# A graph network's neighbour sums: 28 blocks of destinations by matrix product and 21 by gathering, with gathered rows split into three bf16 parts

## The chip, the cores and the metric

The kernel runs on one core of a Trainium2 chip. The time is device microseconds for one execution. Three runs of the kernel before took 2231.62, 2232.75 and 2237.27 us; the median, 2232.75 us, is the time that is compared. The profile is of one further execution.

## The reference

A layer norm and a ReLU turn x (6250 nodes, 256 channels, float32) into h. Then four layers of a graph network follow. Each adds to every node the sum of its neighbours' rows over 100,000 edges (sorted by destination) and applies a three-stage MLP. The last layer's output is added to the input.

```python
def agg(h):
    return jax.ops.segment_sum(h[src], dst, num_segments=N)   # N = 6250
for l in range(NL - 1):                                        # NL = 4
    h = x + agg(x)
    h = jax.nn.relu(h @ W1s[l] + b1s[l])
    h = jax.nn.relu(h @ W2s[l] + b2s[l])
    x = h @ W3s[l] + b3s[l]
h = x + agg(x)
h = jax.nn.relu(h @ cW1 + cb1)
h = jax.nn.relu(h @ cW2 + cb2)                                 # 64 channels
return h @ cW3 + cb3
```

## The kernel before

Nodes are handled in 49 blocks of 128. W1 of a layer is folded into the layer before it (the product of W3 and W1 is made in a preparation of some 145 us), so that the sums are taken over rows that have been multiplied by W1 already, and a layer is: neighbour sums, bias and ReLU, second matrix, bias and ReLU, third matrix, bias.

The neighbour sums of a block of destinations are made in one of two ways.

By product: the lists `panels` name groups of three or four destination blocks. For each panel, a matrix of edge counts (128 sources by 128 destinations for each pair of blocks, kept in DRAM as uint8 in `mats`) is multiplied with all 49 source blocks. The source rows lie in SBUF in `XY` as two float32r halves, a high part and a low part, so that each step (one source block) takes four matmuls: two chunks of channels times two halves (`product`, L1334). Their moving operand is the panel's slice of counts, cast from uint8 by ACT (L1310) or DVE (L1312) into the tile `a`; it is 512 columns wide for four blocks and 384 for three. A panel is 49 such steps. In layer 0 the count matrices are built beside the products out of one-hot matmuls (`build`, L1010), for the panel after the one at work; the last panel, blocks 44 to 47, is not yet there in layer 0.

By gathering: the list `gone` names the blocks that are not in a panel (and blocks 44 to 47, for layer 0 alone). `Gathered.send` (L1183) issues, for each such block, 18 indirect DMAs from GpSimd (L1198). Each brings 128 rows of the layer's table in DRAM, one per edge: nine tiles for each half of 64 destinations. `Gathered.one_hots` makes one-hot matrices of the destinations on DVE (L1223), and `Gathered.add` multiplies them with the rows (L1242). A half of 64 destinations is cut into quarters of 32, following the order of the edges, so that an output of 32 rows is made by a matmul on 32 of TensorE's columns. Rounds pair the tiles of the two quarters; two tiles may belong to both. One call of `add` does three of the six rounds and is called a visit here; a block takes two visits.

Then `finish` adds the block's own row (DVE, L1254), transposes the result (L1264) and hands groups of blocks to `mlp`, as `product` does with its panel. `mlp` spreads its pieces over the following steps with `later` and `due`. The result `zz` is stored to the next layer's table (SP, `rows_io`, L501). Its high and low parts are put in `XY` by `split` (L1055, L1056), directly or after a reload of the row (`back`).

The order on every engine is written out by hand, step by step. `tick` advances one step and runs what is due. A planner spreads the visits over the layer: `when` holds an estimated time for each step, `begin` starts the gathers of a layer as soon as all its table rows have been issued for storing, the first visit comes LEAD units of `when` later, and the last one TAIL steps before the end of the layer. `mlp` keeps its own due time in `free`: a group's second matrix starts at the step after it is handed over or when the group before it leaves room, 5 + (n + 1) // 2 steps apart for the hurried last ones.

Queues: GpSimd issues the gathers; SP issues all other loads and stores of the main part in order (`fetch` L1033, `rows_io` L501 and L506, weights). The gathered rows lie in 24 buffers (layer 0) or 26 (later), and up to two or three visits are sent ahead.

Of the kernel before, what the change touches and what calls it, by code (L numbers as in the profile page):

```python
# [8 lines left out]
F32 = mybir.dt.float32  # L9
# [3 lines left out]
BF16 = mybir.dt.bfloat16  # L13
# [383 lines left out]
def sorted_edges(  # L397
# [57 lines left out]
    CUT = (3, 5)  # L455

    ROUNDS = [(3, 3), (4, 4), (0, 5), (1, 6), (2, 7), (None, 8)]
    EB = -(-E // P)
# [6 lines left out]

    gone = [(0, 4), (4, 4), (8, 4), (12, 4), (16, 3), (44, 4), (48, 1)]
    panels = [(19, 3), (22, 4), (26, 4), (30, 4), (34, 3), (37, 3), (40, 4), (44, 4)]
    S0 = 2 * panels[0][0]
# [21 lines left out]
    eps = const.tile([P, 1], F32, name="eps")  # L490
    tables = [dram.tile([N, C], F32, name=f"table{l}") for l in range(NLAYER + 1)]
    w31d = [dram.tile([P, (KC + 1) * C], F32, name=f"w31_{l}") for l in range(NLAYER)]
    mats = [dram.tile([P, n, NT * P], U8, name=f"mat{p}") for p, (_, n) in enumerate(panels)]
# [407 lines left out]
    with tc.manual_schedule():  # L901
# [36 lines left out]
        def load_weights(l):  # L938
            w2 = load_w("w2", W2s[l] if l < NLAYER else cW2, work, nc.sync)
            if l < NLAYER:  # L940
                w3 = work.tile([P, KC + 1, C], F32, name="w3")
                nc.sync.dma_start(out=w3.rearrange("p k c -> p (k c)"), in_=w31d[l])
            else:
                w3 = late.tile([NOUT, C], F32, name="cw3", bufs=1)
                nc.sync.dma_start(out=w3, in_=cW3)
                row = late.tile([P, C], F32, name="cb3r", bufs=1)
                nc.sync.dma_start(out=row, in_=bass.AP(tensor=cb3.tensor, offset=cb3.offset,
                                                       ap=[[0, P], [1, C]]))
                w3 = (w3, row)
            weights[l] = w2, w3  # L950
# [37 lines left out]
        def build(hots, ats, ps_b):  # L988
# [7 lines left out]
            for k, (p, s, q0) in enumerate(batches):  # L996
# [6 lines left out]
                for q in range(0, BATCH, 2):  # L1003
# [11 lines left out]
                    step += 1  # L1015
                    if step % 4:
                        nc.scalar.copy(o, v)  # L1017
                    else:
                        nc.vector.tensor_copy(o, v)  # L1019
# [22 lines left out]
        def tick():  # L1042
            now[0] += 1
            run = [f for t, f in due if t <= now[0]]
            due[:] = [(t, f) for t, f in due if t > now[0]]
            for f in run:
                f()


# [3 lines left out]
        def split(j, m, z):  # L1053

            nc.scalar.copy(XY[:, j:j + m, :C], z[:, :m, :])  # L1055
            later(1, lambda: nc.vector.tensor_tensor(XY[:, j:j + m, C:], z[:, :m, :],  # L1056
                                                     XY[:, j:j + m, :C].bitcast(F32), OP.subtract))

        def reload(l, j):
# [24 lines left out]
        def mlp(l, b0, n, h1, hurry):  # L1084
# [19 lines left out]
            def third(i):  # L1104
                m = min(2, n - i)
                w3 = weights[l][1]
                if end:
                    xt = late.tile([P, 2, C], F32, name="xt", bufs=3)
                    if b0 + i + m == NT and LAST < P:
# [15 lines left out]
                if end:  # L1125
                    z = late.tile([P, 2, C], F32, name="z", bufs=2)
                    later(2, lambda: nc.vector.tensor_tensor(z[:, :m, :], v, xt[:, :m, :], OP.add))  # L1127
                    later(4, lambda: rows_io(out, b0 + i, m, z, False))
                    return
                z = work.tile([P, 2, C], F32, name="zz", bufs=3)  # L1130
                later(2, lambda: nc.vector.tensor_tensor(  # L1131
                    z[:, :m, :], v, w3[:, KC:, :].to_broadcast([P, m, C]), OP.add))

                def store():
                    rows_io(tables[l + 1], b0 + i, m, z, False)
                    blocks = range(b0 + i, b0 + i + m)
                    kept.update((l, j) for j in blocks)
# [20 lines left out]
        class Gathered:  # L1158
            def __init__(self, l):
                self.l, self.sent, self.done = l, 0, 0  # L1160
                self.first = None
                self.end = ends[l] - TAIL
                self.blocks = [(b, n, i, left[q] + i * T)
                               for q, (b, n) in enumerate(gone) for i in range(n)
                               if l == 0 or (b, n) != panels[-1]]
                self.own = {}
                self.visits = [(g, rounds) for g in range(len(self.blocks)) for rounds in VISITS[l > 0]]
                self.n = len(self.visits)
# [5 lines left out]

            @staticmethod
            def tiles(rounds):
                return sorted({k for r in rounds for k in ROUNDS[r] if k is not None})

            def begin(self, t):
                self.first = when[t] + LEAD  # L1180
                self.pace = (when[self.end] - self.first) / (self.upto[-1] - self.upto[1])

            def send(self, upto):  # L1183
                while self.sent < min(upto, self.n):
# [8 lines left out]
                    for k in self.tiles(rounds):  # L1193
                        for h in range(2):
                            t = gath.tile([P, C], F32, name="rows")
                            self.rows[g, h, k] = t
                            o = self.blocks[g][3] + h * TS + k
                            nc.gpsimd.indirect_dma_start(  # L1198
                                out=t, out_offset=None, in_=tables[self.l][:, :],
                                in_offset=bass.IndirectOffsetOnAxis(ap=idx[:, o:o + 1], axis=0),  # L1200
# [13 lines left out]
            def one_hots(self, v):  # L1214
                g, rounds = self.visits[v]
                o = self.blocks[g][3]
                self.hots = {}
                for r in rounds:
                    hot = work.tile([P, 2, 2, Q], F32, name="hot", bufs=6)
                    for i, k in enumerate(ROUNDS[r]):  # L1220
# [8 lines left out]
            def add(self):  # L1229
# [5 lines left out]
                if v == 0:  # L1235
                    self.one_hots(0)
                end = rounds[-1] == len(ROUNDS) - 1
                for r in rounds:
                    for h in range(2):
                        for m, k in enumerate(ROUNDS[r]):  # L1240
                            if k is not None:
                                nc.tensor.matmul(  # L1242
                                    self.sums[(2 * h + m) * Q:(2 * h + m + 1) * Q, :C],
                                    self.hots[r, m][:, h, :], self.rows[g, h, k], start=(r == 0),
                                    stop=(r == (len(ROUNDS) - 2 if m == 0 else len(ROUNDS) - 1)))
                self.done += 1
# [5 lines left out]
            def finish(self, b, n, g, sums, own):  # L1252
                u = work.tile([P, C], F32, name="u", bufs=1)
                later(1, lambda: nc.vector.tensor_tensor(u, sums[:, :C], own[:, 0, :], OP.add))  # L1254
                if g == 0:
# [27 lines left out]
        ahead = [2, 3]  # L1283
        LEAD, TAIL = 75, 8

        ends = [PRE + NT * sum(k + 1 for k in last[:l + 1]) for l in range(NLAYER + 1)]
        when = [0.0]
        for l, p, _ in units:
            beside = panels[p + 1][1] / 3 if l == 0 and p >= 0 else 0
            when.append(when[-1] + (panels[p][1] + 2 + beside if p >= 0 else 7))  # L1290
        VISITS = [[[0, 1, 2], [3, 4, 5]], [[0, 1, 2], [3, 4, 5]]]
        layers = [Gathered(l) for l in range(NLAYER + 1)]
# [71 lines left out]
        with tc.tile_pool(name="hots", bufs=1) as hots, tc.tile_pool(  # L1364
            name="ats", bufs=1
        ) as ats, tc.tile_pool(name="rings", bufs=AHEAD + 2) as rings, tc.tile_pool(
            name="gath", bufs=24
        ) as gath, tc.tile_pool(
# [17 lines left out]
        late = ctx.enter_context(tc.tile_pool(name="late", bufs=1))  # L1386
        rings = ctx.enter_context(tc.tile_pool(name="rings2", bufs=AHEAD + 4))
        gath = ctx.enter_context(tc.tile_pool(name="gath2", bufs=26))
        ps_a = ctx.enter_context(tc.tile_pool(name="ps_a2", bufs=4, space=PSUM))
# [68 lines left out]
```

## Time and profile before

| | |
|---|---|
| median of three runs | 2232.75 us |
| profiled execution: time / span | 2230.63 us / 2228.8 us |
| TensorE clock granted, mean | 0.983 |
| gathers per layer (0; 1, 2, 3) | 432; 360 |
| products per layer (matmuls; 512 wide / 384 wide) | layer 0: 784 / 588; later: 980 / 588 |
| DMA | 395.56 MB, mean 177 GB/s; queue 0 (GpSimd's) 200.88 MB, 30.2% of 16 engines; queue 1 (SP's) 189.68 MB, 26.8% |
| stages from first gather to last (us) | 144.7 to 713; 746.2 to 1203.5; 1244.4 to 1703; 1741.5 to 2201.5 |
| busy in the stage of layer 1 (457.3 us) | TensorE 450.33, DVE 147.47, ACT 141.91, GpSimd 347.89, DMA share 0.60 |

A line of a group names the code line, the engine, the operation, what is written from what, the shape and the count; then the busy time in us and the mean length in ns of one; then the idle time of the engine just before, and what ended it. A line of a timeline gives the start in us, the length in us, the engine, the line and the operation. PE is TensorE, PEld its weight loads, POOL is GpSimd. An indirect DMA on POOL counts as busy only while it is being issued; its transfer runs on afterwards.

### The profile page before, as it was taken

The numbers are of one execution on the slowest core, as the hardware profiler recorded it, in microseconds if no ns is written. First come the engines' busy times: TensorE is split into PE (matmuls) and PEld (weight loads), VectorE is DVE, ScalarE is ACT, GpSimd is POOL, SyncE is SP. The second block draws the span as 40 slices with busy tenths as digits, with TensorE's granted clock in tenths as the row PEclk, the third lists the DMA queues.
The fourth block names the chain that finished last, engine by engine and source line by source line (L and its number), as shares of the span: only waits on it lengthen the run. The fifth ranks groups of instructions, "written<-read, shape, count | busy, mean of one in ns | idle before, by whom it ended". The sixth has DMA issues, their size and how long they took to land.

```text
span 2228.8 us, 35398 instructions
## 1 busy us (share of the span) xinstructions
PE 2118.0 (95%) x12356; PEld 1559.5 (70%) x12356; DVE 918.2 (41%) x2723; ACT 920.1 (41%) x1915; POOL 1521.5 (68%) x1570
## 2 busy tenths in 40 slices
PE   4778999999999999999999999999999999999998
PEld 2555766667776777778877777778877766677765
DVE  6667465445656522223323422223323423333332
ACT  3666565666667422223334322322324423222222
POOL 2337777777776477777774577777774577777773
PEclk9888999999999999999999999999999999999999
DMA  5436575565666655555655655555655655666663
GB/s 173 134 120 201 185 227 173 178 211 174 200 205 225 195 168 172 165 156 170 193 167 172 191 173 169 157 161 180 187 163 166 204 173 177 184 184 186 191 186 102
DMA packets 264100, 395.56 MB, mean 177 GB/s; under 512 B 36353, under 2 KB 210028, under 8 KB 263912
## 3 DMA queue, kind: packets, MB, share of 16 engines
q0 software_dynamic: 73920, 200.88, 30.2%
q1 hardware_dynamic: 187936, 189.68, 26.8%
q10 hardware_dynamic: 2056, 2.65, 0.4%
q8 instruction: 99, 1.62, 0.3%
q14 instruction: 89, 0.73, 0.1%
HBM read 335.81 MB, written 57.26 MB: 176 GB/s over the span
## 4 chain that ended last, share of the span: by engine, by line
PE 65%; DMA 4%; issue 2%; POOL 1%; ACT 0%; DVE 0%; SPq 0%; POOLq 0%; DVEq 0%
PE agg L1334 45%; PE sums L1242 8%; PE ps L1099 5%; PE ps L1122 4%; DMA rows<-table,idx 3%; POOL rows L1198 1%; PE ps L1119 1%; PE pt L1264 1%; PE bp L1010 1%; DMA xt<-in_x_dram 0%; ACT h L1347 0%; DMA own<-table 0%; DVE z L1127 0%; ACT at L1017 0%; ACT h L1268 0%
## 5 line engine op out<-in xcount | busy, mean ns | idle before, releaser
L1198 POOL DMA_INDIRECT rows<-table,idx x1512 | 1484.3, 982 | 614.0 <-issue 243.5
L1334 PE MATMUL agg<-a,XY 128*128 128x512 f32 (+1 forms) x6076 | 1454.7, 386 | 3.6 <-ACT a L1310 3.2
L1334 PEld LDWEIGHTS agg<-a,XY 128*128 128x128 f32 x6076 | 1085.4, 189 | 239.1 <-issue 81.0
L1310 ACT CAST a<-at 128x512 fp32r<-128x512 uint8 (+1 forms) x943 | 537.0, 579 | 650.3 <-PE agg L1334 585.2
L1312 DVE CAST a<-at 128x512 fp32r<-128x512 uint8 (+1 forms) x576 | 279.6, 490 | 498.7 <-PE agg L1334 455.0
L1242 PE MATMUL sums<-rows,hot 128*32 128x256 f32 x3696 | 281.5, 387 | 31.9 <-DMA rows<-table,idx 30.4
L1242 PEld LDWEIGHTS sums<-rows,hot 128*32 128x32 f32 x3696 | 119.4, 110 | 169.7 <-issue 54.7
L1017 ACT CAST at<-bp 128x392 uint8<-128x392 f32 x348 | 161.1, 490 | 142.8 <-PE bp L1010 139.9
L1099 PE MATMUL ps<-h,w 128*128 128x512 f32 (+5 forms) x392 | 164.3, 541 | 1.2 <-ACT h L1347 1.2
L1254 DVE TENSOR_TENSOR u<-sums,own 128x256 f32<-128x256 f32 x84 | 35.5, 423 | 291.7 <-PE sums L1242 291.7
L1010 PE MATMUL bp<-hi,lo 128*128 128x196 bf16 x928 | 136.0, 259 | 19.9 <-DVE hi L969 11.7
L1223 DVE TENSOR_TENSOR hot<-colf,rel 128x64 f32<-128x64 f32 x924 | 140.6, 217 | 12.3 <-PE sums L1242 11.9
L1122 PE MATMUL ps<-w,h 128*128 128x256 f32 x588 | 140.0, 379 | 0.0
L1010 PEld LDWEIGHTS <-lo 128*128 128x128 bf16 x928 | 71.9, 100 | 94.8 <-issue 43.9
L969 DVE TENSOR_TENSOR lo<-lanes,pairs 128x512 bf16<-128x512 bf16 x232 | 97.1, 419 | 84.0 <-PE bp L1010 58.4
L969 DVE TENSOR_TENSOR hi<-cols,pairs 128x784 bf16<-128x784 bf16 x232 | 129.6, 559 | 0.0
L1122 PEld LDWEIGHTS ps<-w,h 128*128 128x128 f32 x588 | 111.0, 189 | 15.7
L1268 ACT ACTIVATE h<-pt,bias 128x256 f32<-128x256 f32 (+1 forms) x92 | 36.9, 453 | 199.1 <-PE pt L1264 199.1
L1101 ACT ACTIVATE h<-ps,bias 128x512 f32<-128x512 f32 (+5 forms) x98 | 62.4, 637 | 109.6 <-PE ps L1099 109.6
L1131 DVE TENSOR_TENSOR zz<-ps,w 128x512 f32<-128x512 f32 (+1 forms) x81 | 51.7, 638 | 130.9 <-PE ps L1122 130.9
L1099 PEld LDWEIGHTS ps<-h,w 128*128 128x128 f32 (+1 forms) x392 | 68.2, 181 | 51.3 <-issue 29.4
L1019 DVE CAST at<-bp 128x392 uint8<-128x392 f32 x116 | 65.5, 565 | 91.9 <-PE bp L1010 90.3
(134 smaller groups left out, 716.6 us busy)
## 6 DMA issues: line engine op xcount, KB each, us to landing
at<-mat SPq DMA_DIRECT2D x133, 448.0 KB
at<-mat SPq DMA_DIRECT2D x84, 336.0 KB
rows<-table,idx POOLq DMA_INDIRECT x1512
mat<-at SPq DMA_DIRECT2D x29, 784.0 KB
table<-zz SPq DMA_DIRECT2D x66, 256.0 KB
back<-table SPq DMA_DIRECT2D x126, 128.0 KB
own<-table SPq DMA_DIRECT2D x80, 128.0 KB
xs<-in_x_dram SPq DMA_DIRECT2D x8, 768.0 KB
```

The costliest lines, as they stand in the source:

```text
L969: nc.vector.tensor_tensor(o.rearrange("p q (n t) -> p q n t", t=2), values.rearrange("p (n t) -> p n t", t=2)[:, None, :, :].to_broadcast( ...
L1010: nc.tensor.matmul(bp[:, m * HW:(m + 1) * HW], lo[:, q + m, :], hi[:, q + m, :], start=True, stop=True)
L1017: nc.scalar.copy(o, v)
L1019: nc.vector.tensor_copy(o, v)
L1099: nc.tensor.matmul(ps[:mp, :w], weights[l][0][:, c, i * P:i * P + mp], h1[:, c, :w], start=(c == 0), stop=(c == KC - 1))
L1122: nc.tensor.matmul(o, h2[0][:, c, nodes], w3[:, c, :], start=(c == 0), stop=(c == KC - 1))
L1198: nc.gpsimd.indirect_dma_start(out=t, out_offset=None, in_=tables[self.l][:, :], in_offset=bass.IndirectOffsetOnAxis(ap=idx[:, o:o + 1], a ...
L1223: nc.vector.tensor_tensor(hot[:, i, :, :], colf[:, None, i * Q:(i + 1) * Q].to_broadcast([P, 2, Q]), rel[:, o + k:o + k + TS + 1:TS, None] ...
L1242: nc.tensor.matmul(self.sums[(2 * h + m) * Q:(2 * h + m + 1) * Q, :C], self.hots[r, m][:, h, :], self.rows[g, h, k], start=(r == 0), stop= ...
L1310: nc.scalar.copy(o, mat[l, p][j])
L1312: nc.vector.tensor_copy(o, mat[l, p][j])
L1334: nc.tensor.matmul(agg[c][:, :w], XY[:, j, o:o + P], a[:, :w], start=(j == 0 and half == 0), stop=(j == NT - 1 and half == 1))
```

## The change

The blocks are dealt out anew: seven panels of four, blocks 20 to 47, instead of five of four and three of three (19 to 47). Gathered are blocks 0 to 19 and 48 in all layers, and 44 to 47 in layer 0: 25 blocks in layer 0 and 21 in each later one, instead of 24 and 20.

From layer 1 on, the rows that are gathered are no longer float32. When a result `zz` is stored, `in_thirds` also splits each block of it into three bf16 parts (a cast on ACT, a subtraction on DVE, a cast, a subtraction) and stores these, 1.5 KB per row, in a second table `thirds`; `one_step` moves these jobs on at each step, and `finish_thirds` completes them at once where the last results of a layer are stored. A gathered tile is multiplied with one one-hot matrix for 64 destinations, in two bf16 matmuls: the first two parts together (512 columns), then the third (256 columns) on top of the first. A block takes nine rounds, in visits of five and four. DVE adds the two halves of the sum. The one-hot matrices of a visit are made by one instruction. Layer 0 keeps the old way with its float32 rows.

The first visit and the last one of layers 1 to 3 are planned anew (LEAD 90 instead of 75, TAIL 2 instead of 8). The gathered rows lie in 22 buffers, the tiles `a` of the later layers in one buffer less (6 instead of 7 with AHEAD of 3). In the beginning, ACT alone copies the one-hot products out of PSUM.

```diff
-    gone = [(0, 4), (4, 4), (8, 4), (12, 4), (16, 3), (44, 4), (48, 1)]
-    panels = [(19, 3), (22, 4), (26, 4), (30, 4), (34, 3), (37, 3), (40, 4), (44, 4)]
+    gone = [(b, 4) for b in range(0, 20, 4)] + [(44, 4), (48, 1)]
+    panels = [(b, 4) for b in range(20, 48, 4)]
...
+    thirds = [dram.tile([N, 3 * C], BF16, name=f"thirds{l}") for l in range(1, NLAYER + 1)]
...
-                    if step % 4:
+                    if step % 4 or step <= 2 * PRE:
                         nc.scalar.copy(o, v)
...
             for f in run:
                 f()
+            one_step()
...
+        def in_thirds(l, j, z, of):
+            tri = work.tile([P, 1, 3 * C], BF16, name="tri", bufs=2)
+            t = [tri[:, 0, i * C:(i + 1) * C] for i in range(3)]
+            nc.scalar.copy(t[0], z)
+            yield
+            left = work.tile([P, C], F32, name="left", bufs=1)
+            nc.vector.tensor_tensor(left, z, t[0], OP.subtract)
+            yield
+            nc.scalar.copy(t[1], left)
+            yield
+            nc.vector.tensor_tensor(t[2], left, t[1], OP.subtract)
+            rows_io(thirds[l - 1], j, 1, tri, False)
+
+        def one_step():
+            for a in list(thirding):
+                a[1] += 1
+                if next(a[0], True):
+                    thirding.remove(a)
+            if waiting and (not thirding or thirding[-1][1] > 2):
+                a = waiting.pop(0)
+                job = in_thirds(*a)
+                next(job)
+                thirding.append([job, 1, a[3]])
+
+        def finish_thirds(upto):
+            while any(a[-1] <= upto for a in thirding + waiting):
+                one_step()
...
                 def store():
+                    blocks = range(b0 + i, b0 + i + m)
+                    waiting.extend((l + 1, j, z[:, j - b0 - i, :], of) for j in blocks)
+                    if hurry:
+                        finish_thirds(of)
                     rows_io(tables[l + 1], b0 + i, m, z, False)
...
-                self.end = ends[l] - TAIL
+                self.end = ends[l] - (TAIL if l else 8)
...
+                self.rounds = [(k,) for k in range(TS)] if l else ROUNDS
...
-                self.first = when[t] + LEAD
+                self.first = when[t] + (LEAD if self.l else 75)
...
-                            t = gath.tile([P, C], F32, name="rows")
+                            if self.l:
+                                t = gath.tile([P, 3 * C], BF16, name="rows")
+                            else:
+                                t = gath.tile([P, C], F32, name="rows")
...
-                                out=t, out_offset=None, in_=tables[self.l][:, :],
+                                out=t, out_offset=None,
+                                in_=thirds[self.l - 1][:, :] if self.l else tables[0][:, :],
...
+                            if self.l:
+
+                                nc.tensor.matmul(o, self.hots[r, m][:, h, :], t[:, :2 * C],
+                                                 start=(r == 0), stop=False)
+                                nc.tensor.matmul(o[:, :C], self.hots[r, m][:, h, :], t[:, 2 * C:],
+                                                 start=False, stop=stop)
...
-        LEAD, TAIL = 75, 8
+        LEAD, TAIL = 90, 2
...
-        VISITS = [[[0, 1, 2], [3, 4, 5]], [[0, 1, 2], [3, 4, 5]]]
+        VISITS = [[[0, 1, 2], [3, 4, 5]], [[0, 1, 2, 3, 4], [5, 6, 7, 8]]]
...
-            name="gath", bufs=24
+            name="gath", bufs=22
...
-        rings = ctx.enter_context(tc.tile_pool(name="rings2", bufs=AHEAD + 4))
-        gath = ctx.enter_context(tc.tile_pool(name="gath2", bufs=26))
+        rings = ctx.enter_context(tc.tile_pool(name="rings2", bufs=AHEAD + 3))
+        gath = ctx.enter_context(tc.tile_pool(name="gath2", bufs=22))
```

## The prediction

> **What bounds the kernel now.** I read the busy shares first, then the groups kept apart by shape:
>
> ```profile
> PE 2118.0 (95%) x12356; PEld 1559.5 (70%) x12356; DVE 918.2 (41%) x2723; ACT 920.1 (41%) x1915; POOL 1521.5 (68%) x1570
> L1198 POOL DMA_INDIRECT rows<-table,idx x1512 | 1484.3, 982 | 614.0 <-issue 243.5 <-DMA own<-table 112.9 <-PE agg L1334 90.8
> L1334 PE MATMUL agg<-a,XY 128*128 128x512 f32 x3724 | 978.1, 409 | 0.3
> L1334 PE MATMUL agg<-a,XY 128*128 128x384 f32 x2352 | 477.7, 352 | 3.4 <-ACT a L1310 3.2
> L1242 PE MATMUL sums<-rows,hot 128*32 128x256 f32 x3696 | 281.5, 387 | 31.9 <-DMA rows<-table,idx 30.4
> ```
>
> TensorE is busy 95%, GpSimd 68%. The 68% hides a second full engine, as the timeline of GpSimd at the end of layer 0 and of layer 1 shows (start, length, idle before):
>
> ```profile
> 710.63 0.95 POOL L1198 DMA_INDIRECT rows<-table,idx  x1 [0.30 <-issue]
> 711.89 0.95 POOL L1198 DMA_INDIRECT rows<-table,idx  x1 [0.30 <-issue]
> 746.21 0.95 POOL L1198 DMA_INDIRECT rows<-table,idx  x1 [33.38 <-DMA own<-table]
> 747.47 0.95 POOL L1198 DMA_INDIRECT rows<-table,idx  x1 [0.30 <-issue]
> ...
> 1202.48 1.03 POOL L1198 DMA_INDIRECT rows<-table,idx  x1 [0.30 <-issue]
> 1244.45 0.95 POOL L1198 DMA_INDIRECT rows<-table,idx  x1 [40.94 <-DMA own<-table]
> ```
>
> Every gather has 0.30 us before it, whatever releaser is named, so its true price is 1.26 us, and they follow without a pause except at the layer changes. Layer 0: 432 gathers from 144.7 to 711.9, 567.2 us (1.316 each, some stretched). Layers 1 to 3: 360 each, from 746.2, 1244.45 and 1741.6, in 456.3, 457.6 and 458.8 us (up to 1.278 each). With the breaks of 34.3, 42.0 and 39.6 us and 28.4 us from the last gather to the end, the chain of gathers is the whole span: 144.7 + 567.2 + 34.3 + 456.3 + 42.0 + 457.6 + 39.6 + 458.8 + 28.4 = 2228.9. What room GpSimd has is seen where the last gathered matmuls ("visits") of layers 1 and 3 start:
>
> ```profile
> 1217.61 1.50 PE L1242 MATMUL sums<-rows,hot 128*32 128x256 f32 x20
> 2200.42 1.14 POOL L1198 DMA_INDIRECT rows<-table,idx  x1 [0.30 <-PE agg L1334]
> 2202.95 1.62 PE L1242 MATMUL sums<-rows,hot 128*32 128x256 f32 x20
> ```
>
> Layer 1's starts 15.1 us after its last gather, layer 3's 2.5 us, about the flight time; the same subtraction gives 7.2 in layer 0 and 12.5 in layer 2. With 3 us for the flight GpSimd can spare some 4, 12, 10 and 0 us. Both engines are near their limit.
>
> **Gathers, by GpSimd.** Blocks gathered rise from 24 to 25 in layer 0 and from 20 to 21 in the others, at 18 gathers each: 72 more, 1584. Layer 0: 449 periods x 1.316 = 590.9 us. The later ones fetch 1.5 KB per row instead of 1 KB. Near rows, with 98 rows of 1 KB, 72 rows of 0.5 KB, and 98 rows of 5.5 KB:
>
> ```profile
> 40.44 0.97 POOL L680 DMA_INDIRECT wds<-split_e,starts  x1 [0.30 <-issue]
> 71.03 0.95 POOL L741 DMA_INDIRECT near_i<-in_src_dram,from_i  x1 [0.31 <-issue]
> 13.42 1.55 POOL L649 DMA_INDIRECT near_i<-in_dst_dram,at_i  x1 [9.61 <-DVE at_i L628]
> ```
>
> Half a KB costs 0.02 us at most between the first two; the third, an estimate by a straight line, gives (1.55 - 0.97) x 0.5 / 4.5 = 0.06. I take today's 1.275 (1.258 and 1.335 are the ends): 377 x 1.275 = 480.7 us per layer. The Trainium skill, DMA: Bandwidth & Descriptors, section "Issuing engines are not separate DMA queues", says that starting a DMA is usually small beside the DMA itself. Here it isn't: queue 0's 30.2% of the span is 673 us for 1512 gathers, 0.445 us of all engines each against 1.26 of issue. By the rule the gathers would cost what they transfer, 0.67 us at 1.5 times the bytes, still hidden, and the sum would be TensorE's alone; by the row it is GpSimd's. I go by the row. The DMA engines' share, 0.59 to 0.61 in these stages, would rise by 378 x 0.67 / 521 - 360 x 0.445 / 498 = 16 points, and 6 for the thirds' writes: near 80%, not a bound, but flights may lengthen.
>
> **The breaks.** From a last visit to the next first gather takes 27.1, 26.8 and 27.0 us today: 16 steps of the product, the MLPs of block 48 and of the last panel, the store and its flight. In layers 1 and 2 TAIL of 2 puts the visit 6 steps later, but the MLP of block 48 then pushes that of the last panel 6 steps into the next layer: again 16 steps. All are now four blocks wide; eight were three: 32 matmuls x 0.06 = 1.9 us more. The last blocks must also be written as thirds before the next gather: cast, subtract, cast, subtract at some 0.41 us each (the rows of L1055 and L1056), two blocks staggered by three steps of this chain, ahead of the table's store on SP: about 7 x 0.41 = 3 us and a second store in SP's queue and in flight, 5 in all (1 to 8). GpSimd's first gather waits for both, and behind the casts stand the panel's own casts on ACT and DVE. A break thus costs, without slack, 3 + 27 + 1.9 + 5 = 37 us. The tail: 25.9 us today from visit to end; six steps x 4 x 0.237 = 5.7 less, block 48's MLP no longer covered, 1.5 more, 3 of flight: 24.7.
>
> **Sum along GpSimd:** 144.7 + 590.9 + 37 + 480.7 + 37 + 480.7 + 37 + 480.7 + 24.7 = 2313.4.
>
> **TensorE.** The products, from the longest stretches:
>
> ```profile
> 829.45 9.62 PE L1334 MATMUL agg<-a,XY 128*128 128x512 f32 x40
> 1240.28 10.76 PE L1334 MATMUL agg<-a,XY 128*128 128x384 f32 x60
> 604.61 0.51 PE L1010 MATMUL bp<-hi,lo 128*128 128x196 bf16 x4
> ```
>
> Without the last one's drain, 0.237 and 0.177 us apiece. A later layer: 980 x 0.237 + 588 x 0.177 = 336.3 today, 7 panels x 196 x 0.237 = 325.2 after, 11 less; the same in layer 0. Visits today: 1.43 us to the next product's start and 0.09 of the wait before, 1.52, two per block, 3.04; 20 blocks 60.8. A visit of 24 matmuls takes 1.50 us, like one of 20: three rounds in which four groups of 32 columns run side by side. After, each of 18 tiles takes a 512- and a 256-wide bf16 matmul on 64 columns; bf16 runs at 85 ns per 196 columns (0.51 less 0.34 for two, halved), so 0.22 and 0.11. The Trainium skill, TensorEngine Tiling (Array Packing), Theoretical Speedup, allows up to 2 times for 64 columns: 18 x 0.33 / 2 = 2.97, with 0.3 per visit of entry and exit 3.6 per block. But TensorE: Matmul & The Clock Gate, "The mechanism", has matmuls start strictly in order, and the code issues both of one half before the other's: the 256-wide one waits for its own columns and holds the other half back. Then a tile pair takes 2 x 0.22, nine of them 3.96, with exits 4.57. No row has such pairs; I take 4.57, since today's starts are in order too: 21 x 4.57 = 96.0, 35 more per layer (15 by the first rule). A layer of 497.6 us (the mean of two between first gathers), less 4 of waits, becomes 518. GpSimd needs 480.7 + 37 = 517.7.
>
> So both chains ask for the same, and since neither can run far ahead (22 row buffers, 28 gathers in three visits), they cost each other something: today 497.6 where GpSimd alone without slack needs 457 + 30 = 487 and TensorE 494. I add 5 per layer: 2313.4 + 15 = 2328. The measured median lies 3.95 above the span (the profiled execution itself 1.8): **2332 us**.
>
> **At nothing:** one block less to build saves 32 bf16 matmuls (3 us) in layer 0, where the visits wait for gathers anyway; uncovered it is a gain of 3. The thirds' casts within a layer, 49 blocks x 2 x 0.41 = 40 us each on ACT and DVE, fit: these are busy 142 and 147 of 457 us; if they delay a panel's casts, TensorE pays some us. The fewer and wider one-hots lighten DVE. Weights moved from one pool to another, and smaller pools, move no work.
>
> **Rivals.**
> - *Cheap ends.* The price stays at 1.258, thirds hide in the break, the two halves overlap: 2313 - 0.017 x 1131 - 12 + 4 = 2286. For it: the undisturbed period; against: a DMA load near 80%.
> - *Dearer gathers.* 1.335: 2313 + 0.06 x 1131 + 4 = 2385. For it: the 5.5 KB row; against: the flat rows.
> - *TensorE alone, halves don't overlap.* 18 x 0.33 + 0.6 = 6.5 per block: a layer of 518 + 21 x 2 = 560, in all some 2332 + 3 x 38 = 2446. Against: the rounds of four.
> - *Faster.* TensorE is the only bound and the 72 gathers vanish in GpSimd's idle stretches: 2233 - 44 of products + 7 of visits (63 x 3.0 - 60 x 3.04) = 2196. For it: 116 us of breaks and 12 to 15 us before the last visits. It decides from the point where 91 us of gathers fit; I find 26 of slack and 4 in the tail. If the breaks are dependences, as the store before each first gather says, it falls.
>
> **How the numbers follow.** Forecast 0.55 (2305 to 2355); cheap ends 0.20; dearer gathers 0.13; no overlap 0.06; faster 0.04; the change of no effect within the 0.3% that a measurement of this kernel can tell 0.02. The range 2275 to 2390 takes in the first three. Faster 0.04, same 0.02, slower 0.94.
>
> **What would show it.** Right: GpSimd's gathers 1.26 to 1.28 apart in unbroken rows of 378, breaks of 35 to 40 us, last visits 3 to 5 us behind the last gather, TensorE's waits for rows well above 30.4 us, most in layer 0. Wrong: gathers that pause within a layer (TensorE bounds), a period other than 1.26, visits of 3 or 6 us, breaks under 30.

## The result, and the profile after

The changed kernel takes 2350.85 us (median of four runs, 2346.46 to 2354.27), the kernel before 2233.82 us beside it: 1.0521 times, with a 95% interval of 1.0498 to 1.0545. The forecast was 2332 us. The profiled execution took 2349.53 us, its span 2347.7.

The busy shares and the groups of the profile after, in the same columns as before:

```profile
PE 2157.4 (92%) x11192; PEld 1490.3 (63%) x11192; DVE 979.2 (42%) x2438; ACT 980.2 (42%) x2072; POOL 1624.4 (69%) x1642
...
L1247 POOL DMA_INDIRECT rows<-thirds,idx x1134 | 1126.7, 994 | 455.4 <-issue 177.1
L1411 PE MATMUL agg<-a,XY 128*128 128x512 f32 x5292 | 1419.1, 414 | 14.0 <-ACT a L1387 13.4
...
L1247 POOL DMA_INDIRECT rows<-table,idx x450 | 460.5, 1023 | 178.4 <-issue 72.2
...
L1310 PE MATMUL sums<-rows,hot 128*64 128x512 bf16 x1134 | 226.8, 386 | 73.0 <-DMA rows<-thirds,idx 71.8
...
L1312 PE MATMUL sums<-rows,hot 128*64 128x256 bf16 x1134 | 180.0, 274 | 0.0
...
L1315 PE MATMUL sums<-rows,hot 128*32 128x256 f32 x1100 | 92.3, 402 | 17.3 <-DMA rows<-table,idx 17.3
```

TensorE is less busy than before (92% against 95%), in a longer span, and it waits for gathered rows 71.8 + 17.3 = 89.1 us, where it was 30.4. GpSimd's share hardly moved, from 68% to 69%: an undisturbed gather counts as busy for 0.95 us of its 1.26, so that even an unbroken chain of gathers shows only three quarters. Its timeline at the end of layer 1 (start, length, idle before):

```profile
1268.32 1.13 POOL L1247 DMA_INDIRECT rows<-thirds,idx  x1 [0.30 <-issue]
1269.77 0.95 POOL L1247 DMA_INDIRECT rows<-thirds,idx  x1 [0.32 <-issue]
1306.97 1.10 POOL L1247 DMA_INDIRECT rows<-thirds,idx  x1 [36.25 <-DMA back<-table]
1308.37 1.18 POOL L1247 DMA_INDIRECT rows<-thirds,idx  x1 [0.30 <-PE agg L1411]
```

The chain of gathers, laid out as in the prediction from the starts of the first and last gather of each layer, is again the whole span. The last column is after minus before:

| part of the chain | before | predicted | after | after - before |
|---|---|---|---|---|
| to the first gather | 144.7 | 144.7 | 144.6 | -0.1 |
| layer 0: 432, then 450 gathers | 567.2 | 590.9 | 596.4 | +29.2 |
| layers 1 to 3: 360, then 378 gathers each | 456.3, 457.6, 458.8 | 480.7 each | 490.5, 489.3, 489.5 | +96.6 |
| three breaks | 34.3, 42.0, 39.6 | 37 each | 38.3, 37.2, 37.4 | -3.0 |
| last gather to the end | 28.4 | 24.7 | 24.6 | -3.8 |
| sum (span) | 2228.9 | 2313.4 | 2347.8 | +118.9 |

The 72 further gathers at the old mean price (18 at 1.316 us, 54 at 1.275) are 92.5 us of the 118.9. The other 33 us within the layers are nearly all gathers that became longer. The breaks and the end gave 7 us back.

One circumstance of the experiments: in the first ten the kernel before itself took 2857 to 2868 us, because every engine paused again and again there, mostly at the issue of instructions, so these ten are compared as ratios to the kernel before beside them; in the last two it took 2235.06 us.

### The profile page after: what moved, and what is told of

The parts are those of the page before. It is cut to its first block, busy times and chain, and to the rows that moved or that the text cites. A ratio compares the mean times of both kernels' runs of the same rounds, so it can differ in the third digit from the quotient of the medians.

```text
span 2347.7 us, 33135 instructions
## 1 busy us (share of the span) xinstructions
PE 2157.4 (92%) x11192; PEld 1490.3 (63%) x11192; DVE 979.2 (42%) x2438; ACT 980.2 (42%) x2072; POOL 1624.4 (69%) x1642
## 3 DMA queue, kind: packets, MB, share of 16 engines
q10 hardware_dynamic: 2056, 2.65, 0.3%
## 4 chain that ended last, share of the span: by engine, by line
PE 67%; DMA 17%; ACT 4%; issue 4%; DVE 4%; POOL 3%; SPq 0%; ACTq 0%; DVEq 0%; POOLq 0%
PE agg L1411 41%; DMA rows<-thirds,idx 11%; PE ps L1141 6%; PE ps L1164 5%; PE sums L1310 5%; POOL rows L1247 3%; PE sums L1315 2%; DMA thirds<-tri 2%; PE bp L1013 2%; PE sums L1312 2%; DMA rows<-table,idx 1%; PE bp L869 1%; ACT a L1387 1%; ACT at L1020 1%; PE pt L1341 1%
## 5 line engine op out<-in xcount | busy, mean ns | idle before, releaser
L1247 POOL DMA_INDIRECT rows<-thirds,idx x1134 | 1126.7, 994 | 455.4 <-issue 177.1
L1411 PE MATMUL agg<-a,XY 128*128 128x512 f32 x5292 | 1419.1, 414 | 14.0 <-ACT a L1387 13.4
L1387 ACT CAST a<-at 128x512 fp32r<-128x512 uint8 x819 | 500.9, 621 | 557.7 <-PE agg L1411 536.6
L1247 POOL DMA_INDIRECT rows<-table,idx x450 | 460.5, 1023 | 178.4 <-issue 72.2
L1389 DVE CAST a<-at 128x512 fp32r<-128x512 uint8 x504 | 225.5, 451 | 509.2 <-PE agg L1411 491.3
L1310 PE MATMUL sums<-rows,hot 128*64 128x512 bf16 x1134 | 226.8, 386 | 73.0 <-DMA rows<-thirds,idx 71.8
L1312 PE MATMUL sums<-rows,hot 128*64 128x256 bf16 x1134 | 180.0, 274 | 0.0
L1141 PE MATMUL ps<-h,w 128*128 128x512 f32 (+2 forms) x364 | 163.0, 570 | 0.5 <-ACT h L1424 0.5
L1312 PEld LDWEIGHTS <-hot 128*64 128x64 bf16 x1134 | 74.0, 110 | 110.7 <-issue 110.3
L1310 PEld LDWEIGHTS <-hot 128*64 128x64 bf16 x1134 | 70.0, 109 | 89.7 <-issue 40.3
L1315 PE MATMUL sums<-rows,hot 128*32 128x256 f32 x1100 | 92.3, 402 | 17.3 <-DMA rows<-table,idx 17.3
```

Source lines behind the costliest of these rows:

```text
L1141: nc.tensor.matmul(ps[:mp, :w], weights[l][0][:, c, i * P:i * P + mp], h1[:, c, :w], start=(c == 0), stop=(c == KC - 1))
L1247: nc.gpsimd.indirect_dma_start(out=t, out_offset=None, in_=thirds[self.l - 1][:, :] if self.l else tables[0][:, :], in_offset=bass.Indirec ...
L1310: nc.tensor.matmul(o, self.hots[r, m][:, h, :], t[:, :2 * C], start=(r == 0), stop=False)
L1312: nc.tensor.matmul(o[:, :C], self.hots[r, m][:, h, :], t[:, 2 * C:], start=False, stop=stop)
L1315: nc.tensor.matmul(o[:, :C], self.hots[r, m][:, h, :], t, start=(r == 0), stop=stop)
L1387: nc.scalar.copy(o, mat[l, p][j])
```

## The experiments

**What the first ten runs can tell.** The kernel before and the changed kernel, profiled beside the other experiments.

> The kernel before itself, for a profile taken beside the experiments. If it takes about 2857 us as in the timings beside the other runs, every engine pauses where it issues instructions, and GpSimd's 378 gathers of a layer, 1.275 us each (482 us) in the profile of before, spread over about 600 us with pauses of several us at the visits of TensorE; the mean of the gathers that follow without pause stays 1.26 to 1.30 us. If it takes 2233 us, the profile is that of before again.

> The changed kernel itself, timed beside the experiments. If the two parts of the change add up as dealing alone (1.028) and three bf16 parts alone (1.032) suggest, the ratio is 1.060; if the gathers' 480 us a layer hide one part of it, it is the 1.052 of the first result, or lower. If the half of the one-hots does matter, it lies above the 1.051 of the kernel with one-hots in single rounds; if not, within 0.007 of it.

The kernel before took 2863.48 us in its one run, the changed one 3044.49 us, 1.0578 (1.0491 to 1.0664). GpSimd's waits in the kernel before, first as profiled for the prediction, then here:

```profile
POOL rows L1198 <- PE sums L1242: 50.6, 166, 0.3
```

```profile
POOL rows L1198 <- PE sums L1242: 532.4, 139, 15.5
```

In the first, 0.3 us each time is only the step from one gather to the next. In the second, GpSimd stands still for up to 15.5 us until a visit frees its buffers. In layers 1 to 3 I counted the gathers that start within 2.2 us of the one before them apart from those that don't: the first kind starts every 1.272 us in the mean (before) and 1.298 us (after), and the pauses add 319 and 410 us. The profiles above have 1.275 and 1.298, but the agreement of the second number is in part luck. The gathers' own mean length is 0.977 us in the changed kernel here, where it was 0.994, because fewer of them meet one of the long DVE (VectorE) instructions that the last two runs are about; short pauses, too short to be counted as pauses, make up for it. And two runs of one kernel, the dealing alone below, give 1.279 and 1.291 us from start to start, but 0.967 and 0.970 us for the length. So the length of a gather can be compared between these runs, and differences of some 0.01 us from start to start can't. A ratio holds less: GpSimd and TensorE both stand on the path there, and a ratio is uncertain by nearly one per cent.

**The dealing alone**: the kernel before with only the two lists changed, so with float32 rows. It was run twice, on two chips.

```diff
-    gone = [(0, 4), (4, 4), (8, 4), (12, 4), (16, 3), (44, 4), (48, 1)]
-    panels = [(19, 3), (22, 4), (26, 4), (30, 4), (34, 3), (37, 3), (40, 4), (44, 4)]
+    gone = [(b, 4) for b in range(0, 20, 4)] + [(44, 4), (48, 1)]
+    panels = [(b, 4) for b in range(20, 48, 4)]
```

> The new dealing of the blocks alone: seven panels of four and 21 (25) gathered blocks, in float32 as before, with LEAD 75 and TAIL 8. Theory (GpSimd's gathers are the chain): 72 more gathers at some 1.275 to 1.32 us, no slack before the last visits, breaks of 32 us without the thirds: 144.7 + 596 + 33 + 3 x 481 + 2 x 32 + 29 = 2310 us. Rival (TensorE alone bounds): 44 us less of products, 12 more for four blocks' visits: about 2200.

> The kernel of the first experiment once more, since there all engines, of the kernel before too, paused at the issue of instructions, and the times can't be compared with the profiles. As there: GpSimd's gathers as the chain give 144.7 + 596 + 33 + 3 x 481 + 2 x 32 + 29 = 2310 us; TensorE as the only bound gives about 2200.

2946.6 us, 1.0275 (1.0199 to 1.0351), and 2954.23 us, 1.0281 (1.0184 to 1.0377). TensorE has fewer instructions of matmul to do, 11,696 instead of 12,356, and yet the kernel is slower: the theory that TensorE alone paces it, which forecast a faster kernel, is excluded. The loss of 2.8% (79 to 80 us) is near the 72 gathers' 92 us and below the expected 3.5%.

**The three bf16 parts alone**: the changed kernel with the old lists.

```diff
-    gone = [(b, 4) for b in range(0, 20, 4)] + [(44, 4), (48, 1)]
-    panels = [(b, 4) for b in range(20, 48, 4)]
+    gone = [(0, 4), (4, 4), (8, 4), (12, 4), (16, 3), (44, 4), (48, 1)]
+    panels = [(19, 3), (22, 4), (26, 4), (30, 4), (34, 3), (37, 3), (40, 4), (44, 4)]
```

> The bf16 thirds, the 64-wide sums, LEAD, TAIL and buffers of the changed kernel, on the old dealing (20 or 24 gathered blocks). Theory: 432 + 3 x 360 gathers, the later ones 1.30 us as measured in the changed kernel: 144.7 + 567 + 38 + 3 x 467 + 2 x 37.3 + 24.5 = 2250 us. Rival (the thirds themselves are what costs: bigger rows, casts, stores): nearly the whole loss stays, 2330 or more.

2954.89 us, 1.0316 (1.0243 to 1.0389): 0.8% was expected by one theory and 4.4% by the other, and neither is met. The gathers became somewhat longer, 0.976 us in the mean instead of 0.966 (11 us in three layers), but the pauses grew by 88 us, and such pauses within a layer do not occur in the profile after. What the parts cost alone without the pauses is not measured. The two ratios multiply to 1.060, and the whole change has 1.058: the two halves add up within the uncertainty of the ratios.

**Two parts instead of three**: rows of 1 KB, as before the change. The third part isn't stored or gathered; its matmul reads the second part again, so TensorE's work stays and the sums are of less precision.

```diff
-            rows_io(thirds[l - 1], j, 1, tri, False)
+            rows_io(thirds[l - 1], j, 1, tri[:, :, :2 * C], False)
...
-                                t = gath.tile([P, 3 * C], BF16, name="rows")
+                                t = gath.tile([P, 2 * C], BF16, name="rows")
...
-                                nc.tensor.matmul(o[:, :C], self.hots[r, m][:, h, :], t[:, 2 * C:],
+                                nc.tensor.matmul(o[:, :C], self.hots[r, m][:, h, :], t[:, C:],
```

> The changed kernel, but only the first two bf16 parts are stored and gathered (1 KB per row as before); the third matmul reads the second part instead, so the sums lack the third part. TensorE's, ACT's and DVE's work is unchanged. Theory (a fixed price per gather, which stretches for some): between no change, 2350, if the stretched gathers come from elsewhere, and 2320, if the bytes stretch them. Rival (the transfers bound the gathers): a third of the bytes less takes the mean price well below 1.26 or the waits for rows away, under 2300.

3053.47 us, 1.0639 (1.0560 to 1.0719): a third less to fetch brings nothing. The mean length of a gather is 0.979 us, not less than the 0.977 with all three parts. So the bytes are not the cause, neither through the DMA engines nor through the price of a gather; one of the last two runs shows the same without the pauses.

**Sixteen gathers per block**: in layers 1 to 3 the last tile of each half isn't gathered, and its matmuls use the rows of the tile before it. TensorE's work stays. Also run twice.

```diff
                     for k in self.tiles(rounds):
                         for h in range(2):
+                            if self.l and k == TS - 1:
+                                self.rows[g, h, k] = self.rows[g, h, k - 1]
+                                continue
```

> The changed kernel, but of layer 1 on only 16 of each block's 18 tiles are gathered; the ninth tile of each half is multiplied with the eighth's rows, so some edges are left out and others counted twice. TensorE's work is unchanged. Theory (gathers bound): 126 gathers fewer would take 164 us off GpSimd's chain, until TensorE's own floor of some 492 to 497 us per later layer holds: about 2255. Rival (TensorE bounds the changed kernel): no change, 2350.

> The kernel of the fourth experiment once more, for the same reason: of layer 1 on only 16 of 18 tiles are gathered, the ninth of each half is multiplied with the eighth's rows, TensorE's work unchanged. Gathers bound: some 2255 (126 gathers or 164 us less on GpSimd, until TensorE's floor of 492 to 497 us a layer holds). TensorE bound: 2350.

2922.67 us, 1.0170 (1.0075 to 1.0265), and 2899.74 us, 1.0159 (1.0070 to 1.0248), against 1.058 with all 18. Leaving out 126 gathers, worth 126 x 1.298 = 164 us, took 0.041 to 0.042 of 2860 us off, 117 to 120 us. With the same matmuls left, that is GpSimd's price, a little under three quarters of it where the pauses of TensorE stand beside it.

**The order within a visit**: all matmuls of the first 64 columns, then all of the second, for layers 1 to 3.

```diff
-                for r in rounds:
-                    for h in range(2):
+                order = [(r, h) for h in range(2) for r in rounds] if self.l else [
+                    (r, h) for r in rounds for h in range(2)]
+                for r, h in order:
```

> A visit issues all matmuls of the first 64 columns and then all of the second. If TensorE starts a matmul of the other half only within a few instructions of the one that it waits with, the halves no longer overlap: a visit of 5 rounds takes about 5 x (0.216 + 0.108) x 2 = 3.2 us and one of 4 rounds 2.6 us instead of 1.75 and 1.42, 2.65 us a block more, 3 layers x 42 blocks x 2.65 = 334 us more of TensorE's time, and the ratio rises by 0.03 to 0.13. If it takes them in whatever order they are issued, nothing changes (within 0.007 of the changed kernel). In both cases GpSimd's gathers alone keep their mean of 1.30 us.

First a visit of the changed kernel as TensorE's timeline has it (x2 are two matmuls that start together), then a visit in the other order; both have five rounds:

```profile
1078.96 0.41 PE L1310 MATMUL sums<-rows,hot 128*64 128x512 bf16 x2
1079.20 0.28 PE L1312 MATMUL sums<-rows,hot 128*64 128x256 bf16 x2
1079.31 0.39 PE L1310 MATMUL sums<-rows,hot 128*64 128x512 bf16 x2
...
1080.71 0.50 PE L1411 MATMUL agg<-a,XY 128*128 128x512 f32 x1
```

```profile
1065.59 0.40 PE L1311 MATMUL sums<-rows,hot 128*64 128x512 bf16 x1
1065.83 0.27 PE L1313 MATMUL sums<-rows,hot 128*64 128x256 bf16 x1
...
1066.27 0.38 PE L1311 MATMUL sums<-rows,hot 128*64 128x512 bf16 x1
1066.48 0.27 PE L1313 MATMUL sums<-rows,hot 128*64 128x256 bf16 x1
1066.59 0.41 PE L1311 MATMUL sums<-rows,hot 128*64 128x512 bf16 x2
1066.81 0.30 PE L1313 MATMUL sums<-rows,hot 128*64 128x256 bf16 x2
...
1068.34 0.50 PE L1412 MATMUL agg<-a,XY 128*128 128x512 f32 x1
```

The changed kernel issues 512 and 256 of the first half, then 512 and 256 of the second, but the two 512s start together and so do the two 256s: TensorE starts the other half's 512 ahead of a 256 that stands before it and waits for its own columns. Five rounds take 1080.71 - 1078.96 = 1.75 us. In the other order the first three rounds run alone, the fourth and fifth beside the other half's first two, and the visit takes 1068.34 - 1065.59 = 2.75 us. So a matmul is taken ahead over a short distance: the second half's first 512 starts with the first half's fourth, over three matmuls, but not with its third, over five. In the two profiles taken beside each other, the medians of all such visits are 1.75 us and 1.42 us (five and four rounds) in the changed kernel, and 2.75 and 2.10 in the other order: 1.68 us more per block, 63 x 1.68 = 106 us of TensorE's time (the expectation counted visits as blocks there; 63 blocks x 2.65 = 167 us is the amount it should have named). The whole kernel did not become slower for it: 2998.29 us, 1.0406 (1.0306 to 1.0507), against 1.0578 (1.0491 to 1.0664). Why it is rather below, I can't say. A TensorE that sets the pace would have shown 3 to 4% more.

**One-hots made round by round**: the same one-hots made by DVE in instructions of one round (0.28 us) instead of five or four; together they take DVE 162 us instead of 94.

```diff
-                    nc.vector.tensor_tensor(
-                        hot[:, :n, :, :],
...
+                    for i in range(n):
+                        k = rounds[0] + i
+                        nc.vector.tensor_tensor(
+                            hot[:, i, :, :],
...
```

> The changed kernel, with the one-hots of a visit made by one DVE instruction per round (128 elements) instead of one for all five or four (640 or 512 elements, 0.8 and 0.7 us). In the changed kernel 152 of the later layers' gathers ran beside such a one-hot, and took 0.19 us longer on average. Theory: the long DVE instruction with two operands from SBUF stretches the gathers beside it; short ones do less: the mean period of a later layer falls from 1.30 to 1.27 or 1.28, and the time by 20 to 30 us, to 2325. Rival: the larger transfers stretch them: no change.

2995.88 us, 1.0508 (1.0442 to 1.0574). The interval overlaps that of the changed kernel, and the shorter price that was expected did not come: the mean length of a gather is 0.979 us, against 0.977. The stretch (what gathers are longer than 0.955 us, summed) of those beside one-hots was some 7 us, against 11.5 us in the changed kernel beside it, but beside other DVE instructions and alone it grew by more than that. So this run doesn't show that short one-hots make cheaper gathers. It pointed at the one-hots without proving it, so the last two runs take the suspect away and put it in.

**One-hots built once per layer**: those of a layer's first visit are used for all its visits, in layers 1 to 3, so the destinations of the other visits' edges are left out of account; gathers, matmuls and bytes are those of the changed kernel.

```diff
-                    hot = gath.tile([P, 5, 2, 2 * Q], BF16, name="hot", bufs=2)
-                    nc.vector.tensor_tensor(
-                        hot[:, :n, :, :],
...
+                    if v == 0:
+                        self.hot = gath.tile([P, 4, 2, 2 * Q], BF16, name="hot", bufs=1)
+                        nc.vector.tensor_tensor(
+                            self.hot,
...
-                    self.hots = {(r, 0): hot[:, i, :, :] for i, r in enumerate(rounds)}
+                    self.hots = {(r, 0): self.hot[:, i % 4, :, :] for i, r in enumerate(rounds)}
```

> The changed kernel with the one-hots of layers 1 to 3 built once per layer and used for every visit (which destination a row is added to is wrong then; gathers, matmuls and bytes are the same). If the long one-hot instructions of VectorE stretch GpSimd's gathers, the mean of gathers that follow without a pause falls from 1.298 to about 1.275 us in layers 1 to 3 and the gathers' own mean from 0.977 to 0.994 to about 0.965 to 0.970 (1134 x 0.022 = 25 us in all, 0.008 of the ratio, from 1.058 to about 1.050). If the third more of bytes or the writes of the thirds stretch them, both means stay.

**One long one-hot more in the kernel before**: nobody reads its output.

```diff
                 self.hots = {}
+                if self.l:
+                    f, n = (0, 5) if rounds[0] == 0 else (5, 4)
+                    spare = work.tile([P, 5, 2, 2 * Q], BF16, name="spare", bufs=1)
+                    nc.vector.tensor_tensor(
+                        spare[:, :n, :, :],
...
+                            :, f:f + n, :, None].to_broadcast([P, n, 2, 2 * Q]),
+                        OP.is_equal)
```

> The kernel before with one more VectorE instruction per visit in layers 1 to 3, the one-hot of 128 x 640 or 128 x 512 elements of the changed kernel, whose output nobody reads. If it stretches gathers, the mean of gathers that follow without a pause rises from 1.272 to about 1.295 us and the gathers' own mean from 0.966 to about 0.985, the ratio to 1.008 or so; if the bytes or the writes of the changed kernel do, both means stay and the ratio is within 0.005 of 1.

2338.56 us, 1.0455 (1.0431 to 1.0479), for the first: below the changed kernel's 1.0521 by 0.0066, or 15 us, with intervals that don't meet. 2247.28 us, 1.0048 (1.0033 to 1.0062), for the second. The group of the gathers in the two, in this order:

```profile
L1247 POOL DMA_INDIRECT rows<-thirds,idx x1134 | 1104.8, 974 | 457.0 <-issue 162.8
```

```profile
L1198 POOL DMA_INDIRECT rows<-table,idx x1512 | 1516.9, 1003 | 601.1 <-issue 237.1
```

The mean length fell from 994 to 974 ns where the one-hots were taken away, and rose from 982 to 1003 ns where one was put in. In layers 1 to 3, summed from the gathers' own lengths, with each gather put down to the two-operand DVE instruction that it overlaps most:

| | before | one long one-hot more | after | one-hots built once |
|---|---|---|---|---|
| mean length of a gather, us | 0.970 | 0.995 | 0.994 | 0.974 |
| stretch (length above 0.955 us), all gathers, us | 16.2 | 43.1 | 43.8 | 21.8 |
| of it beside one-hots, us | 2.4 | 29.4 | 26.8 | 0.4 |
| mean from start to start, unbroken, us | 1.275 | 1.296 | 1.298 | 1.279 |

The one instruction explains 24.4 of the 27.6 us by which the stretch grew, and putting it in alone makes 27 us of it. With it away, a gather of 1.5 KB rows costs 1.279 us, against 1.275 for 1 KB before. What the gathers gain or lose, the layers do: with the instruction put in, layers 1 to 3 of the kernel before took 10.8, 9.6 and 6.7 us more from their first gather to their last, 27 us in all. Of these 27 us only 12 are in its time (2247.28 against 2235.06 us), because its breaks shrank from 34.3, 42.0 and 39.6 us to 34.3, 34.3 and 34.5: TensorE's last visits had been late, and GpSimd had that room. The 1.0048 by itself would also have met the other theory's "within 0.005"; the gathers' lengths decide.

The one-hots of the kernel before, over all layers, and those of the changed kernel's later layers:

```profile
L1223 DVE TENSOR_TENSOR hot<-colf,rel 128x64 f32<-128x64 f32 x924 | 140.6, 217 | 12.3 <-PE sums L1242 11.9
```

```profile
L1271 DVE TENSOR_TENSOR hot<-colf,rel 128x640 bf16<-128x640 f32 x63 | 51.3, 815 | 0.0
L1271 DVE TENSOR_TENSOR hot<-colf,rel 128x512 bf16<-128x512 f32 x63 | 43.0, 683 | 0.0
```

The 660 short ones of layers 1 to 3 (143 us in all) had 2.4 us of stretch beside them, the 126 long ones (94 us) 26.8. Whether that is for their length or for their bf16 output wasn't separated.

How it happens stands in the timeline of the changed kernel:

```profile
1227.55 0.95 POOL L1247 DMA_INDIRECT rows<-thirds,idx  x1 [0.30 <-DMA rows<-thirds,idx]
...
1228.67 0.80 DVE L1271 TENSOR_TENSOR hot<-colf,rel 128x640 bf16<-128x640 f32 x1
...
1228.81 1.50 POOL L1247 DMA_INDIRECT rows<-thirds,idx  x1 [0.30 <-PE sums L1312]
```

The gather that starts 0.14 us after the one-hot takes 1.50 us instead of 0.95. Sorted by when a gather starts: in the first 0.15 us of a one-hot (42 gathers) it takes 0.46 us more in the mean, between 0.15 and 0.30 us (6) 0.39 us more. Those that started before it run beside most of it and yet take 0.04 us more (up to 0.15 us before, 10 gathers) or 0.17 us (0.15 to 0.30 us before, 17). So it is above all the beginning of a gather's issue that is held up. That the two engines share an access to SBUF would fit the Trainium skill, GPSIMD Engine Reference, section Specifications, which lets GpSimd contend with VectorE where the latter reads two inputs from SBUF; the runs show the delay, not the port.

## Why the prediction was right or wrong

**Gathers set the time, and the gain on the products is lost: right.** The 1584 gathers follow almost without pause in rows of 450 and 378, with GpSimd's chain as the whole span: five pauses in layer 0 and one later, some 7 us in all. Leaving gathers out takes time off, leaving bytes out doesn't, adding work to TensorE's visits doesn't add time, and making gathers longer or shorter makes the layers so.

**The rule and the row for the gather: the row held.** The Trainium skill's rule (DMA: Bandwidth & Descriptors, section "Issuing engines are not separate DMA queues"), by which a DMA's start is usually small beside its transfer, would have made TensorE the bound. The median start-to-start time is 1.258 us with rows of 1.5 KB as it was with 1 KB, and two parts instead of three change nothing.

**The price of a later gather, "I take today's 1.275": mis-sized.** It measured 1.298 us, over 3 x 377 periods 27 us more than predicted, and 5.5 us in layer 0. I had looked for a dearer gather in the bytes and found little, rightly. The cause in the later layers was in a line that I put under "At nothing": "The fewer and wider one-hots lighten DVE". An instruction of 0.67 to 0.86 us holds up the start of a gather where one of 0.22 us hardly did. The one-hots' work on DVE did fall, from 143 to 94 us; the long instructions were what cost. The 5.5 us in layer 0, whose one-hots did not change, are no more than it varies from one execution to another: the last two runs leave it as it is, and it took 600.7 us there against 596.4 in the changed kernel, and 572.8 against 567.2 in the kernel before.

**TensorE's visits, "I take 4.57, since today's starts are in order too": this step failed.** The visits that don't wait for rows take 1.75 + 1.42 = 3.17 us per block, 3.35 with the wait of 0.09 before each, not 4.57. The prediction took a strict order from the Trainium skill (TensorE: Matmul & The Clock Gate, section "The mechanism") and from the starts in the kernel before. Those starts say little on it: the rounds there go through four column groups in turn, so that a blocked matmul has mostly none behind it that could go first. Page and measurement differ, and the measurement decides: TensorE starts a matmul ahead of a blocked one that stands some places before it, so the halves overlap fully, and the value that I worked out from the rule of overlapping columns, 2.97 + 0.6 = 3.57, was the nearer one. "Both chains ask for the same" falls with it. TensorE's busy time and its waits in layer 1, from its first gather to the next layer's (in the first line: the stretch, its length, the busy time and instructions of PE, PEld, DVE, ACT and GpSimd, the granted clock, the DMA share, GB/s):

```profile
779.30:1307.00 527.70, 506.86 (x2494) 360.75 (x2494) 192.87 (x434) 188.73 (x389) 376.53 (x379) 0.99 0.76 234
```

```profile
PE sums L1310 <- DMA rows<-thirds,idx: 15.9, 25, 2.2
PE agg L1411 <- ACT a L1387: 3.9, 3, 1.8
```

Of the stage's 527.7 us TensorE is at work 506.9, and 15.9 of the rest are waits for rows. With visits of 3.35 my sum of 518 would have been 518 - 21 x 1.22 = 492; the other 15 us of TensorE's busy time weren't in it. The trace has them. 14 of the stage's 42 visits are interrupted by a wait for rows, and besides the idle time they keep TensorE busy 13 us longer than undisturbed ones, where in the kernel before such visits cost 4 to 5 us; that leaves some 9 us. And from its first gather to the next layer's, the stage has 1394 products instead of a layer's 1372, an estimated 5.5 us at 0.25 us each.

**The coupling of 5 us per layer: not found.** In layers 1 to 3 the only pause within a layer is one of 1 us. So 15 us were added for a reason that wasn't there, and 33 us of dearer gathers were missing; that the two errors partly cancel, and 2332 came out only 19 us short, was luck: 2313.4 + 27.2 + 5.5 + 1.6 in the breaks and the ends make the span of 2347.7, and the median lies 3.15 above it (3.95 predicted).

**The breaks and the tail: right.** 38.3, 37.2 and 37.4 us for 37, 24.6 for 24.7. That the second store and the thirds' casts share as I put them wasn't tested.

**The DMA share: right.** Near 80% was said, 0.76 and 0.75 are read in layers 1 and 2 (layer 1's stands in the line above), and a third less to fetch brought nothing.

**TensorE's waits for rows: right in size, wrong in place.** 89.1 us is well above 30.4, but only 17.3 of it is in layer 0, where I expected most.

**The rivals.** Cheap ends had the visits right and the price wrong. Dearer gathers had the right direction and the wrong cause: 1.298, not 1.335, and not from bytes. TensorE alone without overlap, and the faster case, fall with the visits and with the dealing alone. Whether the dealing alone would be slower by the same 2.8% without the pauses wasn't measured.

## What to carry to other kernels

An engine that is 68% busy can be the bound: add up its chain, with the fixed gap between its instructions, before believing that work can be moved to it. A long instruction can hold up another engine's start, even where it replaces several short ones and saves its own engine time. Where GpSimd's gathers set the pace, what DVE does beside them has a price per gather, and taking it out is worth a test. Splitting it again isn't shown to help. When two rows can't decide how an engine orders its work, carry both values to the end of the sum.

## What the runs showed of the hardware that I had not expected

- A gather of 128 rows costs GpSimd 0.95 us and 0.30 us before the next, the same for rows of 1 KB and 1.5 KB. A one-hot instruction of 0.67 to 0.86 us on DVE, with two SBUF operands, adds 0.39 to 0.46 us to it in the mean if the gather starts in its first 0.3 us, and less than 0.2 us if the gather starts in the 0.3 us before it.
- TensorE starts a matmul of another column group ahead of one that waits for its own columns: over one matmul in the changed kernel, over three in the other order, but not over five.
- The same kernel took 2233 us in some runs and 2857 us in others. The start-to-start time of unbroken gathers was the same (1.275 and 1.272 us), while TensorE was busy 2333 us instead of 2118, at a granted clock of 0.91 in the mean instead of 0.98. Most of the time was lost in pauses, above all at the issue of instructions, whose cause these runs don't show.
